# Plan, sampling and MLP regrouped into pairs of tiles shifted by one tile, in an attention-plus-deformable-convolution kernel on one Trainium2 core

## The chip, the cores and the metric

The kernel runs on one core of one Trainium2 chip. The metric is the device time of one execution in microseconds: 3890.51 us is the median of three runs (3889.94 to 3891.61). All arithmetic is in float32.

## The reference

The input is four images of 64 x 64 pixels with 256 channels. Each image goes through two blocks. The first is self-attention over all 4096 pixels of the image, the second a transformer-like block whose spatial step is a deformable convolution with 16 groups of 16 channels and 3 x 3 points.

```python
q, k, v = x @ wq, x @ wk, x @ wv                     # 32, 32 and 256 wide
x = x + gamma * softmax(q @ k.T) @ v                 # 4096 x 4096 in each image
h = ln(x)                                            # layer norm 1
proj = h @ inproj                                    # what is sampled
t = gelu(ln(depthwise3x3(h)))                        # 9 taps, per channel
offset, mask = t @ off_w, softmax(t @ mask_w)        # 16 groups x 9 points
s = sum over points of mask * bilinear(proj, point + offset)
x = x + s @ outproj
x = x + gelu(ln(x) @ fc1) @ fc2                      # 1024 hidden
```

(Biases are left out.) The offsets are small in nearly all places, so the kernel takes the bilinear sample from a window of 5 x 5 pixels around each pixel, with weights (hats) that are zero outside. The few points that fall outside the window are repaired afterwards, in a "far round".

## The kernel before, in words

**Tiles and units.** A tile is 128 pixels, two image rows. A unit is two tiles, 256 pixels. There are 16 units in an image and 64 in all. Everything is done unit by unit, in stages:

- *project* (L407 to L442): q, k and v of one unit of the *next* image: transposes pt_x, the copy xT on ScalarE, the matmuls pkq and pv. Image 0's projection comes ahead of everything.
- *attention* (L502 to L527): scores e in four groups e0 to e3 of 16 matmuls, exponentials ex (steps x0 to x3, four ScalarE instructions each, L515), and the products acc with V (steps w0 to w15 of 8 matmuls each). acc lies in PSUM, two tiles of 257 columns.
- *front* (L543): division by the softmax sum (L550), the residual, layer norm 1 (xn_f, nm_f), transposes pt_f, hT_f, the input projection pp and its store xq to the DRAM tensor xp. Its step scale also stores hT_f to a DRAM image himg (L573).
- *plan* (L607): loads six rows of himg into hs (L613), computes the nine taps into cv (tap 0 on ScalarE, L624, the others on VectorE, L628), transposes to pc, layer norm (xn_p, with rstd_p on GpSimd), gelu, the heads po (L662) and om, the hats, the mask weights, their products pr (L751) and the window weights wn. Its step count puts into cnt how many far points the unit has, with two ScalarE operations named far. It stores am and om to DRAM for the far round.
- *sample* (L830): reads window rows of xp (win) and forms the weighted sum with multiplications (times, L842) and additions (plus, L850, then three across), once per tile and window row. Result sp.
- *back* (L960, which calls finish, L875): transposes pt_s, the output projection pout (L895), the residual x1b, layer norm 2 (xn_b), transposes pt_b, the hidden layer ph (hidden0 to hidden7, L919) with gelu into gT (L927), the second layer pmlp (L936), the store of the output.
- *far round* (L997) once at the end: picks for each of 128 rows a unit with far points, gathers am, om, the table values, four neighbours (nears), sp and x1, and runs them through finish as one tile more. The checks at the end need it.

**Order.** The order is written by hand. `whole` (L1118) gives every step the time slot x 60 + WHEN[stage][step], sorts all steps and emits them in that order, and each of TensorE, VectorE, ScalarE and GpSimd runs its instructions in just that order. SyncE issues the transfers in the same order. Slots are nominal; in the profile a slot takes what its engines need. Attention of unit s has slot s, its front s+1, its plan s+2, its sample and back s+3. So in a steady slot TensorE mixes work of four units and of the next image's projection.

**Buffers.** pt of every kind, ph, pp, pv, pkq, pmlp, pc, po and pout take turns in one PSUM pool of two buffers: each of these tiles can be written only when the one before the last has been read. ScalarE must load another function table when it changes between gelu and exponential; the steps gelu0, gelu1 and exp place a dummy operation (idle, L301) so that the load stands at a chosen place.

The slots of the last stages are set in these lines of `whole`:

```python
put(s + 1, "front", front(att))
put(s + 2, "plan", plan(b, u, wns, general))
put(s + 3, "sample", sample(b, u, wns, sps))
put(s + 3, "back", back(b, u, sps))
```

Of the kernel before, what the change touches and what calls it, by code (L numbers as in the profile page):

```python
# [16 lines left out]
def tile_attention_dcnv3_block(  # L17
# [20 lines left out]

    nc = tc.nc
# [4 lines left out]
    NU = N // 256  # L44
    CQ = wq.shape[1]
# [11 lines left out]
    out_ = out.rearrange("b (t q h2) w c -> b t (h2 w) q c", q=2, h2=2)  # L57
# [110 lines left out]
    himg = []  # L168
    for b in range(B):
        for y in (0, H + 2):  # L170
            nc.gpsimd.dma_start(
                xp[b, y : y + 2].rearrange("y w c -> (y w c)").rearrange("(p f) -> p f", p=P),
                zeros[:, : 2 * WP * C // P],
            )
        for w in (0, W + 2):
            nc.gpsimd.dma_start(
                xp[b, 2 : 2 + H, w : w + 2, :].rearrange("y w c -> y (w c)"), zeros[:H, : 2 * C]
            )
        h = dram.tile([P, C // P, H + 2, W], F32, tag=f"himg{b}", name=f"himg{b}")
        for y in (0, H + 1):  # L180
            nc.gpsimd.dma_start(h[:, :, y, :], zeros[:, : 2 * W].rearrange("p (k w) -> p k w", k=2))
        himg.append(h)

    hs = gp.tile([P, C // P, 6, WP], F32, name="hs")
# [4 lines left out]
    omd = dram.tile([B * NU * P, 2 * NOM], F32, name="omd")  # L189

    amd = dram.tile([B * NU * P, 2 * S], F32, name="amd")
    x1d_ = x1d.rearrange("(u q p) c -> u p q c", q=2, p=P)
    spd_ = spd.rearrange("(u q p) c -> u p q c", q=2, p=P)
    omd_ = omd.rearrange("(u p) m -> u p m", p=P)
    amd_ = amd.rearrange("(u p) m -> u p m", p=P)
# [3 lines left out]

    UN = B * NU  # L200
    tab_s = dram.tile([2 * S, 4], F32, name="tab_s")
    tab_u = dram.tile([UN, 2], F32, name="tab_u")
# [9 lines left out]
    byp = tab[0:1, : 8 * S].rearrange("p (s f) -> p s f", f=4)  # L212
# [3 lines left out]
    numbers(byp[:, :, 3], [[1, 2], [0, S]], 0)  # L216
    nc.vector.scalar_tensor_tensor(byp[:, :, 2], byp[:, :, 3], 2.0, byp[:, :, 2], ALU.mult, ALU.add)
    nc.gpsimd.dma_start(tab_s.rearrange("(o s) f -> o (s f)", o=1), tab[0:1, : 8 * S])
    tab = p1.tile([P, 2 * S], F32, tag="mk", name="tab_b")
    byu = tab[0:1, : 2 * UN].rearrange("p (s f) -> p s f", f=2)  # L220
    numbers(byu[:, :, 0], [[H + 4, B], [0, NU]], 0)
    numbers(byu[:, :, 1], [[0, B], [4, NU]], 0)
    nc.gpsimd.dma_start(tab_u.rearrange("(o s) f -> o (s f)", o=1), tab[0:1, : 2 * UN])
# [9 lines left out]
    rev = gp.tile([P, UN], F32, name="rev")  # L233
    numbers(rev, [[-1, UN]], UN)
# [4 lines left out]
    cnt = gp.tile([P, B * NU], F32, name="cnt")  # L239
# [8 lines left out]
    qd = dram.tile([B * NU, CQ, 256], F32, name="qd")  # L248
# [3 lines left out]
    rall = gp.tile([P, B * NU, 2], F32, name="rall")  # L252
# [53 lines left out]
    def transposed(src, name, n=2, pool=None, tag="m"):  # L306

        pt = (pool or ps).tile([P, C // P, 256], F32, tag=tag, name=f"pt_{name}")
        for k in range(C // P):
# [15 lines left out]
            "load": -8.0, "turn": 14.59, "copy": 19.06, "keys": 20.23, "key_bias": 21.3, "values": 24.48,  # L325
            "value_bias": 27.18,
        },
        "attention": {
            "load": -20.0, "e0": -5.48, "x0": -3.77, "e1": 1.23, "w0": 3.99, "w1": 6.55, "w2": 8.71,
            "w3": 18.86, "x1": 20.1, "e2": 24.15, "x2": 24.96, "w5": 27.12, "e3": 30.32, "w11": 32.05,  # L330
            "w8": 34.09, "w6": 41.58, "w9": 45.95, "w7": 46.83, "w4": 48.34, "x3": 49.31, "w10": 53.77,
            "w12": 54.23, "w14": 54.57, "w13": 56.92, "w15": 60.51,
        },
        "general": {
            "e0": -0.1, "x0": 0.0,
        },
        "tables": {
            "gelu0": -3.72, "gelu1": 34.44, "exp": 43.95,
        },
        "front": {  # L340
            "inverse": 0.67, "residual": 1.94, "stats": 3.81, "shift": 4.26, "norm": 6.3, "turn": 8.65,
            "scale": 10.32, "project_in": 20.46, "store": 24.02, "keep": 37.44,
        },
        "plan": {
            "load": -32.0, "tap0": -4.53, "tap1": -4.08, "tap2": -1.32, "tap3": -0.19, "tap4": 7.76,
            "row": 12.0, "tap5": 16.0, "tap6": 25.94, "tap7": 25.95, "tap8": 25.98, "turn": 28.86,
            "stats": 31.74, "shift": 34.62, "norm": 37.78, "turn2": 39.37, "gelu": 43.09, "heads0": 44.15,
            "bias0": 44.78, "heads1": 44.8, "bias1": 45.25, "mask_exp": 46.47, "hat0": 46.5, "hat2": 48.1,
            "sums": 49.15, "hat1": 49.55, "invert": 50.34, "weigh": 52.55, "nearer": 52.63, "near": 52.66,
            "bounds": 53.75, "mask0": 53.9, "mask1": 54.13, "count": 54.63, "product0": 55.35,  # L350
            "y_copies0": 55.98, "y0": 57.71, "product1": 57.78, "y1": 59.2, "y_copies1": 60.27,
            "x_copies": 60.38, "x": 63.91,
        },
        "sample": {
            "rows01": 4.08, "times01": 4.1, "rows00": 4.39, "times00": 4.41, "rows02": 5.83, "times02": 5.85,
            "plus01": 7.59, "plus02": 10.32, "rows03": 11.62, "times03": 11.64, "rows04": 16.49,
            "times04": 16.51, "plus03": 19.73, "plus04": 24.86, "rows11": 25.7, "times11": 25.72,
            "across00": 25.8, "across01": 28.32, "rows12": 29.39, "times12": 29.41, "across02": 31.4,
            "rows10": 33.28, "times10": 33.3, "plus11": 34.57, "plus12": 37.6, "rows13": 42.08,
            "times13": 42.1, "rows14": 43.6, "times14": 43.62, "plus13": 44.73, "plus14": 46.89,  # L360
            "across10": 49.5, "across11": 50.19, "across12": 51.27,
        },
        "back": {
            "load": 30.0, "turn": 52.73, "copy": 53.52, "project_out": 54.04, "added": 55.57, "stats": 57.22,
            "shift": 57.89, "norm": 59.56, "turn2": 61.2, "scale": 61.21, "raised": 61.31, "hidden0": 62.08,
            "hidden4": 62.46, "gelu0": 63.21, "hidden2": 64.68, "gelu4": 64.68, "gelu2": 64.99,
            "hidden6": 65.94, "hidden1": 67.15, "gelu6": 67.4, "gelu1": 68.64, "hidden5": 69.49,
            "hidden3": 72.49, "gelu5": 72.71, "gelu3": 72.87, "hidden7": 73.81, "gelu7": 77.75,
            "narrowed0": 84.81, "narrowed1": 89.91, "end": 93.7,
        },  # L370
        "far": {
            "unit": -84, "point": -80, "left": -77, "rows": -76, "pixels": -74, "summed": -66, "turn": 34.5,
            "copy": 35.11, "project_out": 35.71, "added": 36.32, "stats": 36.93, "shift": 37.54,
            "norm": 38.14, "turn2": 38.75, "scale": 39.36, "raised": 39.96, "hidden0": 40.57,
            "hidden4": 41.18, "gelu0": 41.79, "hidden2": 42.39, "gelu4": 43.0, "gelu2": 43.61,
            "hidden6": 44.21, "hidden1": 44.82, "gelu6": 45.43, "gelu1": 46.04, "hidden5": 46.64,
            "hidden3": 47.25, "gelu5": 47.86, "gelu3": 48.46, "hidden7": 49.07, "gelu7": 49.68,
            "narrowed0": 50.29, "end": 50.89,
# [164 lines left out]
    def front(att):  # L543
# [26 lines left out]
        def scale():  # L570
            st["hT"] = scaled(st["pt"], g1, b1, f"f{n}")
            for k in range(C // P):
                nc.sync.dma_start(  # L573
                    himg[b][:, k, 1 + 4 * u : 5 + 4 * u, :],
                    st["hT"][:, k, :].rearrange("p (r w) -> p r w", w=W),
                )
# [14 lines left out]
        def store():  # L591
# [11 lines left out]
            "project_in": project_in, "store": store, "keep": keep,  # L603
# [3 lines left out]
    def plan(b, u, wns, general):  # L607
        n = f"{b}_{u}"
        st = {}

        def load(r0, r1):
            for k in range(C // P):
                nc.sync.dma_start(  # L613
                    hs[:, k, r0:r1, 2 : 2 + W], himg[b][:, k, 4 * u + r0 : 4 * u + r1, :]
                )


        def tap(j, k):
            if (j, k) == (0, 0):
                st["cv"] = p1.tile([P, C // P, 256], F32, tag="cv", name=f"cv_{n}")  # L620
            acc = st["cv"][:, k, :].rearrange("p (r w) -> p r w", w=W)
            src = hs[:, k, j // 3 : j // 3 + 4, 1 + j % 3 : 1 + j % 3 + W]
            if j == 0:
                nc.scalar.activation(  # L624
                    acc, src, AF.Identity, bias=dwb[:, k : k + 1], scale=dw[:, k, 0:1]
                )
            else:
                nc.vector.scalar_tensor_tensor(acc, src, dw[:, k, j : j + 1], acc, ALU.mult, ALU.add)  # L628

        def taps(j):  # L630
            tap(j, 0)
            tap(j, 1)

        def turn():
            st["pc"] = ps.tile([P, 2, C], F32, tag="m", name=f"pc_{n}")
            for i in range(2):
# [5 lines left out]
        def stats():  # L642
            statistics(st, [st["pc"][:, i, :] for i in range(2)], f"p{n}")

        def norm():
            normalised(st, [st["pc"][:, i, :] for i in range(2)], f"p{n}")

        def turn2():
            st["pt"] = transposed(st["xn"], f"p_{n}")
# [589 lines left out]
```

## Time and profile before

| quantity | value |
|---|---|
| median of three runs | 3890.51 us |
| the profiled execution | 3889.96 us |
| its span | 3888.1 us |
| a slot of images 0 to 2 in the steady state | 58.2 us |
| a slot of image 3 (no next image to project) | 55.7 us |
| last product with V ends, about | 3691.3 us |

In the profile PE is TensorE and PEld its weight loads, DVE is VectorE, ACT ScalarE, POOL GpSimd, SP SyncE. A row of a timeline gives the start and the length in us, the engine, the line of the kernel, the operation, the tiles written and read (out<-in), the shape, how many instructions were taken together, and in brackets how long the engine had been idle and what ended that. Matmul ends are modelled, so the start of one row to the start of the next is a better measure than a row's length. The busiest groups of the page are these; the last columns are busy us and mean ns of one instruction, then the idle time before them:

```profile
L527 PE MATMUL acc<-V,ex 128*128 128x257 f32 x8192 | 1903.3, 382 | 0.0
...
L842 DVE TENSOR_TENSOR pw<-win,wn 128x1280 f32<-128x1280 f32 x640 | 937.1, 1482 | 7.0 <-ACT gT L927 0.4
L850 DVE TENSOR_TENSOR pw<-pw,pw 128x1280 f32<-128x1280 f32 x512 | 759.2, 1483 | 0.2
L515 ACT ACTIVATE ex<-e 128x512 f32<-128x512 f32 x1024 | 527.4, 600 | 214.3 <-PE e L502 206.7
```

### The profile page before, as it was taken

What the parts mean: (1) busy time and instruction counts of PE and PEld (TensorE: products, weight loads), DVE (VectorE), ACT (ScalarE), POOL (GpSimd) and SP (SyncE); (2) the same over time, 40 slices, a digit from 0 to 9 for tenths busy, and PEclk for the clock granted to TensorE, in tenths of its full rate; (3) what the DMA queues carried; (4) which work ended last, traced back from release to release, by engine and by line L of the source; (5) the groups of instructions that cost most, each with busy time, mean ns of one, the idle gap of its engine ahead of it and who ended that gap; (6) DMA issues with size and microseconds to landing.
All of it is one profiled execution on the core that took longest, in us unless ns stands there. A gap on an engine that the chain in (4) does not pass through costs nothing.

```text
span 3888.1 us, 56223 instructions
## 1 busy us (share of the span) xinstructions
PE 3783.9 (97%) x20284; PEld 3120.9 (80%) x20284; DVE 3413.4 (88%) x6157; ACT 1996.0 (51%) x3986; POOL 320.0 (8%) x445
## 2 busy tenths in 40 slices
PE   8999999999999999999999999999999999999946
PEld 7878888888888888888888888888888888888834
DVE  2399989989989989989989989999999999999995
ACT  4555555555555555555555555555555555555522
POOL 2000000000000000000000000000000000000020
PEclk9999999999999999999999999999999999999977
DMA  5343343335343334334444334334435333433331
GB/s 148 91 117 100 107 111 103 104 111 149 102 131 106 102 110 107 100 111 120 132 130 110 99 109 111 99 108 113 135 99 129 97 101 99 107 97 103 93 89 32
DMA packets 352352, 419.95 MB, mean 108 GB/s; under 512 B 137312, under 2 KB 302368, under 8 KB 352064
## 3 DMA queue, kind: packets, MB, share of 16 engines
q1 hardware_dynamic: 341904, 409.42, 39.0%
q10 hardware_dynamic: 8512, 3.43, 0.4%
q8 instruction: 162, 2.65, 0.3%
q0 software_dynamic: 1648, 3.40, 0.3%
q14 instruction: 126, 1.03, 0.1%
HBM read 276.86 MB, written 139.27 MB: 107 GB/s over the span
## 4 chain that ended last, share of the span: by engine, by line
PE 95%; DVE 4%; DMA 1%; issue 0%; ACT 0%; POOL 0%; SPq 0%; POOLq 0%; ACTq 0%; DVEq 0%
PE acc L527 46%; PE ph L919 11%; PE pmlp L936 11%; PE e L502 7%; PE po L662 5%; PE pv L434 3%; PE pout L895 3%; PE pp L586 3%; PE pkq L413 1%; DVE pw L842 1%; PE pc L638 1%; PE pt_s L311 1%; PE pt_p L311 1%; PE pt_f L311 1%; PE pt_b L311 1%; PE pt_x L311 1%
## 5 line engine op out<-in xcount | busy, mean ns | idle before, releaser
L527 PE MATMUL acc<-V,ex 128*128 128x257 f32 x8192 | 1903.3, 382 | 0.0
L527 PEld LDWEIGHTS acc<-V,ex 128*128 128x128 f32 x8192 | 1528.5, 190 | 261.0 <-issue 64.8
L842 DVE TENSOR_TENSOR pw<-win,wn 128x1280 f32<-128x1280 f32 x640 | 937.1, 1482 | 7.0 <-ACT gT L927 0.4
L850 DVE TENSOR_TENSOR pw<-pw,pw 128x1280 f32<-128x1280 f32 x512 | 759.2, 1483 | 0.2
L515 ACT ACTIVATE ex<-e 128x512 f32<-128x512 f32 x1024 | 527.4, 600 | 214.3 <-PE e L502 206.7
L919 PE MATMUL ph<-hT_b,f1w 128*128 128x256 f32 x2048 | 496.5, 386 | 3.2 <-ACT hT_b L291 2.7
L927 ACT ACTIVATE gT<-ph,f1b 128x256 f32<-128x256 f32 x512 | 241.2, 471 | 478.2 <-PE ph L919 478.2
L936 PE MATMUL pmlp<-f2w,gT 128*128 128x256 f32 x2048 | 466.6, 381 | 0.0
L919 PEld LDWEIGHTS ph<-hT_b,f1w 128*128 128x128 f32 x2048 | 384.8, 192 | 80.9 <-issue 20.1
L628 DVE SCALAR_TENSOR_TENSOR cv<-hs,dw,cv 128x256 f32<-128x256 f32 x1024 | 436.7, 478 | 6.3 <-ACT cv L624 6.3
L936 PEld LDWEIGHTS pmlp<-f2w,gT 128*128 128x128 f32 x2048 | 384.6, 191 | 54.9 <-issue 5.3
L283 ACT ACTIVATE xn_p<-pc,nm_p,rstd_p 128x256 f32<-128x256 f32 x128 | 65.2, 560 | 615.6 <-DVE nm_p L275 615.6
L502 PE MATMUL e<-qs,kT 32*128 32x256 f32 x4096 | 305.5, 402 | 0.7 <-ACT ex L515 0.7
L502 PEld LDWEIGHTS e<-qs,kT 32*128 32x128 f32 x4096 | 191.9, 184 | 86.2 <-issue 53.1
L301 ACT ACT_TABLE_LOAD x192 | 246.3, 1283 | 2.6
L269 POOL TENSOR_SCALAR rstd_p<-mv_p 128x2 f32<-128x2 f32 x64 | 81.5, 1274 | 1562.3 <-DVE mv_p L267 1562.3
L662 PE MATMUL po<-om_w,ge 128*128 128x432 f32 x512 | 199.4, 533 | 1.3 <-ACT ge L655 1.3
L751 DVE TENSOR_TENSOR pr<-hat 128x1296 f32<-128x1296 f32 x128 | 192.5, 1504 | 6.7
L593 DVE TENSOR_TENSOR xq<-pp,inb 128x512 f32<-128x512 f32 x64 | 44.2, 691 | 138.8 <-PE pp L586 138.8
L662 PEld LDWEIGHTS po<-om_w,ge 128*128 128x128 f32 x512 | 98.5, 193 | 73.0 <-issue 57.2
L434 PE MATMUL pv<-wv_s,xT 128*128 128x256 f32 x512 | 127.7, 393 | 4.0 <-DVE V L442 4.0
L269 POOL TENSOR_SCALAR rstd_b<-mv_b 128x2 f32<-128x2 f32 x64 | 20.8, 325 | 1311.7 <-DVE mv_b L267 1290.7
(211 smaller groups left out, 3683.4 us busy)
## 6 DMA issues: line engine op xcount, KB each, us to landing
win<-xp SPq DMA_DIRECT2D x536, 320.0 KB, 4.5
omd<-om SPq DMA_DIRECT2D x64, 432.0 KB, 2.8
hs<-himg SPq DMA_DIRECT2D x128, 160.0 KB, 3.1
xs<-in_x_dram SPq DMA_DIRECT2D x64, 256.0 KB, 2.9
x<-in_x_dram SPq DMA_DIRECT2D x64, 256.0 KB, 2.9
himg<-hT_f SPq DMA_DIRECT2D x128, 128.0 KB, 2.9
xp<-xq SPq DMA_DIRECT2D x128, 128.0 KB, 2.4
x1d<-x SPq DMA_DIRECT2D x64, 256.0 KB, 3.2
```

The source lines that it names most:

```text
L301: nc.scalar.activation(idle, minus_half[:, 0:1], func)
L434: nc.tensor.matmul(pv[:, i, :], lhsT=st["xT"][:, k, i * P : (i + 1) * P], rhs=wv_s[:, k, :], start=(k == 0), stop=(k == 1),)
L502: nc.tensor.matmul(es[r][:, jj, :], lhsT=self.kT[2 * g + jj][rows4(r), :], rhs=self.qs[rows4(r), :], start=True, stop=not self.general,)
L515: nc.scalar.activation(ex, self.es[r], AF.Exp)
L527: nc.tensor.matmul(self.acc[i], lhsT=ex[:, jj, i * P : (i + 1) * P], rhs=V[t // 2][:, t % 2, :], start=(g == 0 and r == 0 and jj == 0), st ...
L628: nc.vector.scalar_tensor_tensor(acc, src, dw[:, k, j : j + 1], acc, ALU.mult, ALU.add)
L662: nc.tensor.matmul(st["po", i], lhsT=st["ge"][:, k, i * P : (i + 1) * P], rhs=om_w[:, k, :], start=(k == 0), stop=(k == 1),)
L842: nc.vector.tensor_mul(st[r].rearrange("p d (g c) -> p (d g) c", c=GC), src.rearrange("p d (g c) -> p (d g) c", c=GC), wns[b, u][:, i, r] ...
L850: nc.vector.tensor_add(st[0], st[0], st[r])
L919: nc.tensor.matmul(ph[:, :m], lhsT=f1w[:, k, c * P : (c + 1) * P], rhs=st["hT"][:, k, :m], start=(k == 0), stop=(k == 1),)
L927: nc.scalar.activation(st["gT"][:, c, :m], st["ph", c][:, :m], AF.Gelu, bias=f1b[:, c : c + 1])
L936: nc.tensor.matmul(po, lhsT=st["gT"][:, c, i * P : (i + 1) * P], rhs=f2w[:, c, :], start=(c == 0), stop=(c == NH - 1),)
```

## The change

Attention and front still go by units. Plan, sample and back go by pairs v = 0 to 64: pair v holds the tiles 2v-1 and 2v, so pairs 0 and 64 hold one tile each, and a pair at a border of images (v = 16, 32, 48) holds the last tile of one image and the first of the next. Pair v needs pixel rows only up to the first half of unit v and one row more, which front of unit v yields. Plan of pair v has slot v+1, the slot of that front, and sample and back have slot v+2.

The DRAM image himg goes, with its stores, loads and zero fills. hs has seven rows and stays in SBUF: the new step image copies hT_f into rows 3 to 6 on ScalarE, and the new step carry moves the rows 4 to 6 down to 0 to 2 after the taps. The centre tap comes first and is the one on ScalarE. A tap that would read over the border of two images is cut in two. am, om and the window weights are stored by pairs, with four zero fills for the missing tiles of pairs 0 and 64; the far round picks pairs, and reads the image and row of a tile from a table by tiles, with one more small gather moved from its step pair to point.

All times in WHEN are new, for project and attention too. Among them: pt_x stands between hidden2 and hidden4, and pv ahead of pkq; hidden3 comes late, after most of the products with V; count comes in the next slot, among the gelus. With the new places of gelu and exponential there are six table loads in a steady slot instead of four.

```diff
+    def tiles_of(v):
+        return max(2 * v - 1, 0), 1 if v in (0, UN) else 2
...
-    hs = gp.tile([P, C // P, 6, WP], F32, name="hs")
+    hs = gp.tile([P, C // P, 7, WP], F32, name="hs")
...
         "project": {
-            "load": -8.0, "turn": 14.59, "copy": 19.06, "keys": 20.23, "key_bias": 21.3, "values": 24.48,
-            "value_bias": 27.18,
+            "load": -14.4, "turn": 19.72, "copy": 23.24, "values": 37.05, "value_bias": 42.74, "keys": 48.45,
+            "key_bias": 50.49,
...
         "tables": {
-            "gelu0": -3.72, "gelu1": 34.44, "exp": 43.95,
+            "gelu0": -12.71, "gelu1": 13.84, "exp": 41.13,
...
-            "shift": 57.89, "norm": 59.56, "turn2": 61.2, "scale": 61.21, "raised": 61.31, "hidden0": 62.08,
-            "hidden4": 62.46, "gelu0": 63.21, "hidden2": 64.68, "gelu4": 64.68, "gelu2": 64.99,
-            "hidden6": 65.94, "hidden1": 67.15, "gelu6": 67.4, "gelu1": 68.64, "hidden5": 69.49,
-            "hidden3": 72.49, "gelu5": 72.71, "gelu3": 72.87, "hidden7": 73.81, "gelu7": 77.75,
-            "narrowed0": 84.81, "narrowed1": 89.91, "end": 93.7,
+            "shift": 59.05, "norm": 59.26, "raised": 59.37, "turn2": 59.4, "scale": 59.75, "hidden0": 59.78,
+            "hidden5": 61.44, "gelu0": 65.24, "gelu5": 67.65, "hidden1": 68.95, "gelu1": 70.18,
+            "hidden2": 73.18, "gelu2": 77.76, "hidden4": 81.06, "gelu4": 84.59, "hidden6": 84.61,
+            "hidden7": 87.12, "gelu6": 87.36, "gelu7": 93.93, "hidden3": 99.62, "gelu3": 101.35,
+            "narrowed0": 102.2, "narrowed1": 106.29, "end": 106.65,
...
         def scale():
             st["hT"] = scaled(st["pt"], g1, b1, f"f{n}")
-            for k in range(C // P):
-                nc.sync.dma_start(
-                    himg[b][:, k, 1 + 4 * u : 5 + 4 * u, :],
-                    st["hT"][:, k, :].rearrange("p (r w) -> p r w", w=W),
-                )
+
+        def image():
+            nc.scalar.copy(hs[:, :, 3:, 2 : 2 + W], st["hT"].rearrange("p k (r w) -> p k r w", w=W))
...
+            dy = j // 3 - 1
+            parts = [(0, 4)]
+            if v % NU == 0 and dy:
+                parts = [(0, 2), (3, 4)] if dy < 0 else [(0, 1), (2, 4)]
+            r0 = 2 if v == 0 else 0
+            for a, b in parts:
+                a, b = max(a, r0), min(b, r0 + 2 * nt)
+                if a >= b:
+                    continue
+                src = hs[:, k, a + 1 + dy : b + 1 + dy, 1 + j % 3 : 1 + j % 3 + W]
+                dst = acc[:, a - r0 : b - r0, :]
...
+        def carry():
+            nc.scalar.copy(hs[:, :, :3, 2 : 2 + W], hs[:, :, 4:, 2 : 2 + W])
...
-                put(s + 2, "plan", plan(b, u, wns, general))
-                put(s + 3, "sample", sample(b, u, wns, sps))
-                put(s + 3, "back", back(b, u, sps))
+        for v in range(PN):
+            put(v + 1, "plan", plan(v, wns, general))
+            put(v + 2, "sample", sample(v, wns, sps))
+            put(v + 2, "back", back(v, sps))
...
-            put(B * NU + 2, "far", far_round(B * NU - 3))
-            put(B * NU + 2, "checks", checks)
+            put(UN + 2, "far", far_round(UN - 3))
+            put(UN + 2, "checks", checks)
```

## The prediction

> **What bounds the kernel now.** I read the page's totals, slices and chain first, then a table of two typical stretches, then single rows where two numbers did not fit, then the tail.
>
> ```profile
> span 3888.1 us, 56223 instructions
> ...
> PE 3783.9 (97%) x20284; PEld 3120.9 (80%) x20284; DVE 3413.4 (88%) x6157; ACT 1996.0 (51%) x3986; POOL 320.0 (8%) x445
> ...
> PEclk9999999999999999999999999999999999999977
> ...
> PE 95%; DVE 4%; DMA 1%; issue 0%; ACT 0%; POOL 0%; SPq 0%; POOLq 0%; ACTq 0%; DVEq 0%
> ```
>
> TensorE holds 95% of the chain, and no queue or transfer holds more than 1%: only what shortens PE's own sequence, or PE's waits at the two ends, can move the time. The profiled run took 3889.96 us, 1.9 over its span and 0.55 under the median; the sum below is made on 3889.96.
>
> The next view is busy time by stage: one attention slot of image 1 and one of image 3.
>
> ```profile
> 1520.49:1578.71 58.22, 58.22 (x318) 48.27 (x317) 52.90 (x94) 30.86 (x63) 4.40 (x6) 1.00 0.38 106
> ...
> 3302.59:3358.30 55.71, 55.71 (x301) 45.91 (x300) 52.31 (x93) 29.30 (x59) 4.40 (x6) 1.00 0.38 101
> ```
>
> The columns are length, busy PE, PE's weight loads, DVE, ACT and POOL, granted clock, DMA share and GB/s. PE fills both slots, and DVE has 5.3 and 3.4 us left. An image-3 slot lacks the next image's projection: pt_x 0.44, pkq 0.86 and pv 1.73 us from start to start, 3.03 in all. It is only 2.51 shorter, so 0.52 us hide in it. The timeline of PE (start, us) shows where; one row from either slot, and the one after:
>
> ```profile
> 1539.60 1.15 PE L502 MATMUL e<-qs,kT 32*128 32x256 f32 x16
> ...
> 3320.40 1.67 PE L502 MATMUL e<-qs,kT 32*128 32x256 f32 x16
> 3322.00 3.72 PE L936 MATMUL pmlp<-f2w,gT 128*128 128x256 f32 x16
> ```
>
> Start to start the same 16 matmuls take 1.08 us in image 1 and 1.60 in image 3. ScalarE's timeline gives the reason:
>
> ```profile
> 3317.05 0.47 ACT L927 ACTIVATE gT<-ph,f1b 128x256 f32<-128x256 f32 x1 [0.39 <-PE ph L919]
> 3317.53 1.28 ACT L515 ACT_TABLE_LOAD   x1
> 3318.82 2.06 ACT L515 ACTIVATE ex<-e 128x512 f32<-128x512 f32 x4
> ```
>
> The four exponentials of e1 end at 3320.88, and e2 needs the PSUM they free. Without the projection PE is there too early, and waits inside a row that counts as busy.
>
> The tail, from the last acc (3691.3) to the end at 3888.1, is 196.8 us. Its windows and waits of PE:
>
> ```profile
> 3700.00:3750.00 50.00, 19.81 (x69) 13.62 (x68) 43.45 (x112) 6.57 (x13) 18.37 (x14) 0.74 0.37 91
> 3750.00:3800.00 50.00, 28.91 (x93) 20.32 (x93) 47.33 (x80) 16.11 (x33) 4.36 (x5) 0.78 0.30 83
> ...
> 3850.00:3889.00 39.00, 22.77 (x91) 17.83 (x89) 3.95 (x10) 6.48 (x13) 2.04 (x3) 0.82 0.06 20
> ```
> ```profile
> PE pt_s L311 <- DVE sp L859: 15.4, 3, 9.9
> PE pt_b L311 <- ACT xn_b L283: 15.0, 4, 6.0
> PE pc L638 <- DVE cv L628: 14.8, 2, 7.7
> PE pt_s L311 <- DVE om L671: 9.2, 1, 9.2
> ```
>
> Here DVE leads, PE waits for it, and PE's granted clock falls to 0.74 to 0.82.
>
> **The change part by part.** All sums follow the changed order of each engine, with the durations of the rows of before.
>
> *A steady slot: PE.* Plan, sample and back keep their matmuls; only their grouping into units moves by a tile. The floor stays 58.2 us with the projection and 55.2 without, and PE's order has no operation more. Cost 0 as long as each producer ends before PE asks.
>
> *A steady slot: DVE.* 64 taps of 256 elements and all else stay; a tap is cut in two only at the four image borders. 53 us against 58.2 is cover enough. In image 3 it is 52.5 against 55.2; without that cover each us of DVE over 55.2 would cost 16.
>
> *A steady slot: ACT.* Added: the copy of hT into the row buffer (128x512; the like copy xT takes 0.58) and the carry of three rows (384 elements, between us 0.31 and xT 0.58, so 0.45), and table loads go from 4 to 6 a slot (the order alternates more between gelu and exp), 2.57. ACT rises from 31 to 35 us of 58, with most of it beside PE.
> Here a rule speaks against the change. The Trainium skill ("ScalarE: Activation LUTs", section "What ACT_TABLE_LOAD costs") charges a switch with the 1283 ns load and a further 1380 ns of drain, 2.66 in all. The rows above show the load starting 0.01 us after gT ends, and the first exponential 1.29 after the load starts: no drain is seen. By the row the first gelu of a slot is ready 0.7 us before ph1 asks for its buffer (ledger: 4.45 against 5.17 us after pt_b). By the rule it would be 1.4 later, 0.7 too late in 64 slots: +45 us. I take the row.
>
> *A steady slot: PSUM.* ph, pt, pc, po, pp, pv, pout, pkq and pmlp share two buffers in turn, so each waits until the one before the last was read. In the new order pt_x stands amid the hidden layers, and ph6 must wait for the copy xT, which queues on ACT behind gT1, two far counts (0.54 and 0.44), a table switch's idle (0.20), gT2 and two xn_f (0.52 each at pitch). The ledger ends xT at 9.65 to 9.9 us after pt_b, and PE wants ph6 at 9.94. Behind ph6 all of PE's slot queues. Bounds: the 0.52 us of the one ACT wait of this kind in the trace, and −0.24, because PE's pitches add up to 57.97 of the 58.22 and the new order might save the difference. As the estimated slack is 0 to 0.3, I take +0.05 a slot, in the 48 slots with a projection: +2.4. The other slacks in the ledger are 0.2 to 0.5 us (heads after gelu, pt_s after sp, pout after sT): 0.
>
> *Image 3.* The exponentials of e1 now end 3 to 5 us before e2 asks, since e2 stands later in the order. The 0.52 goes in 16 slots: −8.3. Next late is po after ge, 0.3 us of slack.
>
> *Transfers.* The DRAM image goes: 128 stores (128 KB, 2.9 us to land) and 128 loads with their row loads (160 KB, 3.1). They lay beside PE with queues at 39%: gain 0. Plan, sample and back take their transfers with them (am, om, the window rows, sp, x1, out); in SP's order none of these stands in front of a load that is due earlier: 0, and if one did, times, with 5 us of DVE's room in a slot, would hide it. Eight zero fills by GpSimd become four, before the first slot: 0.
>
> *The head.* DVE-bound slots fill the pipeline. The slot at 186.5 to 239.8 took 53.3 us, and its PE records add up to 43.7 at pitch: 9.6 lost. With plan one slot earlier, taps delay pc by about 5.6 in slot 2, and slot 3 (PE 50.9, DVE 53.5) loses 2.6: 8.2. Gain 1.4, with 0.5 of waits for xn_p that no longer occur: −1.9, bounds −5 to +3.
>
> *The tail and what leaves it.* When the last acc ends there remain 3.5 backs, 2.5 samples and 1.5 plans instead of 4, 3 and 2. Half a pair's PE work therefore moves ahead of it: 32 matmuls of the MLP at 0.217 (6.9), half of pout 0.87, one po 1.45 and transposes 0.9 to 1.0: +10.2 in a stretch that PE fills. The tail of before by its DVE rows: to the add of f2b at 3762.06 70.3 us; to the next at 3812.82 50.8; to the end of the last sum 40.2; the last back 26.6; its end 8.5 and 0.4 between.
> After: the first stretch keeps two tiles everywhere (70.1), but the plan's rstd queues on POOL behind four gathers of the far round: POOL is busy 18.4 us in that window, and my queue count makes nm_p about 3.3 late, so 73.4. The second has half a plan: 42.2 of DVE records, and 5.1 of waits (pout at the low clock 3.1, twice 0.5, and 1.1): 47.3. Then the MLP of pair 63 is the path and no longer DVE, 19.2; the far round's one-tile back 16.3 (18.0 in before, 1.7 of it a wait for DVE); the last back has one tile and is like the far one, 17.0 instead of 26.6; end 8.5. Sum 181.7 against 196.8: −15.1, bounds −18 to −10.
>
> Sum: 3889.96 + 2.4 − 8.3 − 1.9 + 10.2 − 15.1 = 3877.3, and 0.55 to the median: **3878 us**, 0.3% faster.
>
> **The rivals.**
> *The stall moves instead of going.* In image 3 DVE has 2.7 us left and po 0.3. If a new wait of 0.52 takes the place of the old, −8.3 is lost; with xT at 0.1 a slot (+2.4 more) it ends at 3889. For it: every link in the order is tight. Against it: the largest known wait has 3 us of slack.
> *The xT copy decides; slower.* If ph6 waits 0.52 a slot, the size that image 3 shows for an ACT wait, 48 × 0.52 = 25 instead of 2.4: 3901. It turns the gain into a loss from 0.31 us a slot (15/48). For it: no slack in the ledger and three ACT operations of another stage ahead. Against it: the sum uses whole durations, and gT rows follow each other at 0.44 or less.
> *The tail does better.* No wait on POOL (−3.3), no wait for xT (−2.4), the second stretch without its pout wait (−3.1), the head at −5: 3866; two us more if part of the 0.24 falls away.
>
> **How the numbers follow.** A change of 0.2%, 7.8 us, is about what a measurement of this kernel can tell from none: 3882.7 and 3898.3 are the borders. The likeliest case has 0.58 (3870 to 3886 with the tail's, head's and xT's bounds), the better tail 0.14, the moved stall 0.18, the slow case 0.10. Faster: most of the first, 0.54, and the second, with 0.06 of the third: 0.74. Slower: most of the fourth, 0.08. The rest, 0.18, is within. The range from 3864 to 3889 leaves the slow case and half of the moved stall out.
>
> **What would show it.** Slots of 58.2 in images 0 to 2 (58.7 would be the slow case, and ph6 rows long by 0.5) and 55.2 in image 3, with e2 at 1.15 us; 6 table loads a slot with ex 1.29 after the load's start; no himg transfers; the last acc near 3694 (3691.3 + 10.2 + 2.4 − 8.3 − 1.9); then about 182 us of tail, with the far chain behind the MLP of pair 63. The prediction fails if a slot is not PE's, or if the new tail is led by something that I took for covered, POOL above all.

## The result, and the profile after

The changed kernel takes 3876.2 us (median of six runs, 3874.87 to 3878.25) against 3890.41 us (six runs, 3888.19 to 3891.61): a ratio of 0.9964, 95% interval 0.9951 to 0.9977. The forecast was 3878. The profiled execution has a span of 3874.4 us and took 3876.21.

The page of the changed kernel, the lines that answer to those of before:

```profile
span 3874.4 us, 55924 instructions
...
PE 3777.5 (97%) x20316; PEld 3125.1 (81%) x20316; DVE 3424.4 (88%) x6224; ACT 2204.0 (57%) x4262; POOL 317.5 (8%) x444
...
PEclk9999999999999999999999999999999999999977
...
PE 94%; DVE 4%; DMA 1%; issue 0%; ACT 0%; POOL 0%; ACTq 0%; POOLq 0%; DVEq 0%
```

ScalarE is 208 us busier and the chain has not noticed: it is still 94% PE. Busy time by stage, one slot of image 1 and one of image 3 (length, busy PE, PEld, DVE, ACT, POOL, clock, DMA share, GB/s):

```profile
1531.50:1589.71 58.21, 58.21 (x317) 48.38 (x316) 53.07 (x94) 34.13 (x66) 4.40 (x6) 1.00 0.34 95
3364.03:3419.22 55.19, 55.19 (x302) 45.72 (x301) 52.20 (x93) 32.60 (x62) 4.41 (x6) 1.00 0.32 90
```

The first slot is as long as before, to 0.01 us, with 3.3 us more on ScalarE. The second is 0.52 shorter. Its row of e2 on TensorE, and on ScalarE the exponentials of e1 that it needs:

```profile
3383.57 1.15 PE L506 MATMUL e<-qs,kT 32*128 32x256 f32 x16
3384.65 2.00 PE L531 MATMUL acc<-V,ex 128*128 128x257 f32 x8
```
```profile
3376.80 0.47 ACT L936 ACTIVATE gT<-ph,f1b 128x256 f32<-128x256 f32 x1
3377.28 1.28 ACT L519 ACT_TABLE_LOAD   x1
3378.57 2.06 ACT L519 ACTIVATE ex<-e 128x512 f32<-128x512 f32 x4
```

The exponentials end at 3380.6, and TensorE comes 2.9 us later: e2 takes 1.08 us from start to start, no longer 1.60. The table load again starts 0.01 us after the gelu ends, and the exponential 1.29 after that.

The tail, from the end of the last acc (3694.8) to 3874.4, is 179.6 us, 17.2 shorter. Its windows and TensorE's waits in it:

```profile
3700.00:3750.00 50.00, 24.44 (x81) 16.94 (x80) 44.99 (x112) 10.28 (x21) 19.06 (x14) 0.69 0.34 86
3750.00:3800.00 50.00, 28.66 (x91) 19.59 (x89) 48.48 (x87) 16.29 (x36) 4.19 (x5) 0.76 0.24 67
3800.00:3850.00 50.00, 35.75 (x145) 27.82 (x145) 28.22 (x58) 14.81 (x35) 3.05 (x5) 0.76 0.06 19
```
```profile
PE pc L648 <- DVE cv L635: 19.3, 2, 13.9
PE pt_b L316 <- ACT xn_b L288: 13.9, 3, 5.4
PE pt_p L316 <- ACT xn_p L288: 12.1, 2, 8.9
PE pt_s L316 <- DVE sp L868: 7.1, 2, 4.5
```

VectorE leads until 3800, and is only 28 us busy in the third window: there the chain of MLPs leads. Over the whole tail VectorE's busy time fell from 148.5 to 128.3 us, as half a pair less to do would have it.

### The profile page after: what moved, and what is told of

It reads as the page before. It is cut to its first block, busy times and chain, and to the rows that moved or that the text cites. A ratio compares the mean times of both kernels' runs of the same rounds, so it can differ in the third digit from the quotient of the medians.

```text
span 3874.4 us, 55924 instructions
## 1 busy us (share of the span) xinstructions
PE 3777.5 (97%) x20316; PEld 3125.1 (81%) x20316; DVE 3424.4 (88%) x6224; ACT 2204.0 (57%) x4262; POOL 317.5 (8%) x444
## 4 chain that ended last, share of the span: by engine, by line
PE 94%; DVE 4%; DMA 1%; issue 0%; ACT 0%; POOL 0%; ACTq 0%; POOLq 0%; DVEq 0%
PE acc L531 46%; PE ph L928 11%; PE pmlp L945 11%; PE e L506 7%; PE po L672 5%; PE pout L904 3%; PE pv L438 3%; PE pp L588 3%; PE pkq L417 1%; DVE pw L851 1%; PE pt_s L316 1%; DVE pw L859 1%; PE pt_p L316 1%; PE pt_b L316 1%; PE pc L648 1%; PE pt_f L316 1%
## 5 line engine op out<-in xcount | busy, mean ns | idle before, releaser
L928 PE MATMUL ph<-hT_b,f1w 128*128 128x256 f32 (+1 forms) x2080 | 497.8, 383 | 4.2 <-ACT hT_b L296 2.5
L635 DVE SCALAR_TENSOR_TENSOR cv<-hs,dw,cv 128x256 f32<-128x256 f32 (+1 forms) x1076 | 427.6, 462 | 7.5 <-ACT cv L631 1.5
L288 ACT ACTIVATE xn_p<-pc,nm_p,rstd_p 128x256 f32<-128x256 f32 x128 | 65.4, 560 | 608.2 <-DVE nm_p L280 608.2
L936 ACT ACTIVATE gT<-ph,f1b 128x256 f32<-128x256 f32 (+1 forms) x520 | 236.2, 467 | 241.2 <-PE ph L928 240.0
L506 PE MATMUL e<-qs,kT 32*128 32x256 f32 x4096 | 295.7, 401 | 0.7 <-ACT ex L519 0.7
L274 POOL TENSOR_SCALAR rstd_p<-mv_p 128x2 f32<-128x2 f32 (+1 forms) x65 | 80.4, 1237 | 1680.3 <-DVE mv_p L272 1680.2
L665 ACT ACTIVATE ge<-pt_p,bd,gd 128x256 f32<-128x256 f32 (+1 forms) x130 | 65.9, 558 | 161.3 <-PE pt_p L316 161.3
L672 PEld LDWEIGHTS po<-om_w,ge 128*128 128x128 f32 x512 | 98.5, 193 | 72.8 <-issue 64.4
L681 DVE TENSOR_TENSOR om<-po,om_b 128x432 f32<-128x432 f32 x128 | 77.4, 604 | 88.2 <-PE po L672 88.2
```

Of the source, the lines that this page charges most:

```text
L506: nc.tensor.matmul(es[r][:, jj, :], lhsT=self.kT[2 * g + jj][rows4(r), :], rhs=self.qs[rows4(r), :], start=True, stop=not self.general,)
L635: nc.vector.scalar_tensor_tensor(dst, src, dw[:, k, j : j + 1], dst, ALU.mult, ALU.add)
L672: nc.tensor.matmul(st["po", i], lhsT=st["ge"][:, k, i * P : (i + 1) * P], rhs=om_w[:, k, :], start=(k == 0), stop=(k == 1),)
L928: nc.tensor.matmul(ph[:, :m], lhsT=f1w[:, k, c * P : (c + 1) * P], rhs=st["hT"][:, k, :m], start=(k == 0), stop=(k == 1),)
L936: nc.scalar.activation(st["gT"][:, c, :m], st["ph", c][:, :m], AF.Gelu, bias=f1b[:, c : c + 1])
```

## The experiments

Theory: the time is 16 image-3 waits that are gone, and a tail with half a pair less to do, minus the half pair of TensorE work that moved ahead of it; the other slots, the transfers and ScalarE's extra work are neutral. Rivals: the lighter queues bring part of it; the image-3 gain comes from the grouping and not from a wait; the PSUM turn at ph6 is not the edge it was taken for.

**e2 later, in the kernel before.**

```diff
-"e2": 24.15, "x2": 24.96
+"e2": 24.9, "x2": 24.96
```

> The kernel before with one number changed: e2 moves behind the first half of the second layer (and behind pv), so that TensorE reaches it 3.5 us later and the exponentials of e1 have ended. Theory (a wait for x1 hides in each image-3 slot): image-3 slots go from 55.70 to 55.18, slots of images 0 to 2 stay at 58.21, time 3890.4 - 15 or 16 x 0.52 = 3882.4. Rival (the shorter image-3 slot of the changed kernel comes from the regrouping into pairs, or from the transfers that are gone): slots stay at 55.70 and the time at 3890.

Measured: 3937.9 us, 47 slower. The image-3 slots did fall, to 55.40. But images 0 to 2 rose to between 59.3 and 59.4, which I had not expected. There pv moved ahead of e2 too, and now met the PSUM turn: it waits for qT, the reader of pkq, which stands behind the exponentials. The same row in the timeline of TensorE:

```profile
1569.48 1.99 PE L434 MATMUL pv<-wv_s,xT 128*128 128x256 f32 x8 [0.79 <-ACT qT L427]
```

A swap of two steps that are both "not waiting" costs 1.1 us a slot. So the edit was repeated for image 3 alone:

```diff
+                if b == B - 1:
+                    steps.append((s * T + 24.9, len(steps), some.pop("e2")))
                 put(s, "attention", some)
```

> The kernel before with e2 moved behind the first half of the second layer in image 3 alone, so that the projection's use of the PSUM buffers in images 0 to 2 is not touched. In the run that moved it everywhere the image-3 slots came to 55.40. Theory (a wait for the exponentials of e1 hides there; 0.22 of its 0.52 us turn up again at pc, which then waits for VectorE's last taps): slots of 58.21 and 55.40, 3890.5 - 16 x 0.31 = 3885.6. Rival (nothing hides there): 3890.5.

Measured: 3886.3 us (3882.8 to 3888.6), ratio to before 0.9990 (0.9982 to 0.9998); slots are 58.21 and 55.40, as expected. The wait is real and has nothing to do with pairs. TensorE's rows there show where the rest stays:

```profile
3375.34 1.15 PE L502 MATMUL e<-qs,kT 32*128 32x256 f32 x16
3376.41 2.00 PE L527 MATMUL acc<-V,ex 128*128 128x257 f32 x8
3378.25 0.81 PE L638 MATMUL pc<-ident,cv 128*128 128x128 f32 x4
3378.90 3.40 PE L936 MATMUL pmlp<-f2w,gT 128*128 128x256 f32 x15
```

e2 now takes 1.07, but pc 0.65 from start to start and not 0.44: it waits for the last taps on VectorE, whose row ends at 3378.46. In the old order 0.31 of the 0.52 was to be had; the changed kernel, whose taps come early, has all of it.

**The copy xT, later in the changed kernel**, by one operation or by waiting for ph4.

```diff
-"carry": 60.61
+"carry": 82.0
```

> The changed kernel with the step carry (0.51 us on ScalarE, 0.42 at pitch) moved from before the slot's gelus to just ahead of the copy xT. The trace of the changed kernel has xT end 9.6 us after pt_b and ph6 start at 9.94, a slack of 0.33. Theory (the second user of a PSUM buffer is the sharp edge of the new order, as the slow rival of the prediction had it): 0.42 less 0.33 is 0.1 us of wait or, with the latency of the semaphore, up to 0.2, in 48 slots: 3876.2 + 5 to 10 = 3881 to 3886, slots of images 0 to 2 at 58.3 to 58.4, image 3 unchanged at 55.18. Rival (the wait is taken up by TensorE's queue or the slack is larger than it looks): 3876.

Measured: 3887.1 us (3885.4 to 3891.5), 10.9 more, which gives back three quarters of the gain; the ratio to the kernel before is 0.9993 (0.9985 to 1.0001). Slots of images 0 to 2 are 58.46, 0.25 longer, and 48 x 0.25 = 12. On ScalarE (in this kernel's slot pt_b began at 2706.87) and on TensorE:

```profile
2715.91 0.51 ACT L642 COPY hs<-hs 128x384 f32<-128x384 f32 x1
2716.32 0.58 ACT L411 COPY xT<-pt_x 128x512 f32<-128x512 f32 x1
```
```profile
2714.20 1.90 PE L531 MATMUL acc<-V,ex 128*128 128x257 f32 x8
2715.94 3.01 PE L928 MATMUL ph<-hT_b,f1w 128*128 128x256 f32 x12
2718.78 0.60 PE L316 MATMUL pt_f<-ident,xn_f 128*128 128x128 f32 x4
```

No idle time is printed; the wait sits inside ph's row, 2.84 us from start to start and not 2.59. As 0.42 of delay cost 0.25, the changed kernel had 0.17 us in hand. The slow rival's mechanism is real; it does not bind by 0.17 us.

```diff
-"copy": 23.24
+"copy": 24.6
```

> The changed kernel with the copy xT moved behind gelu4 on ScalarE. gelu4 must wait for ph4, which ends 9.94 us after pt_b, so xT ends near 11.2 and ph6, which TensorE reaches at 9.94, can start near 11.4. Theory (that buffer is the edge): 1.4 us in each of 48 slots, 3876.2 + 67 = 3943, slots of images 0 to 2 at 59.6. Rival (another operation of TensorE's order fills in, or later waits shrink by as much): well under 30 us more.

Measured: 3911.9 us, 35.7 more, half of the 67 expected. Slots are 59.05, 0.83 longer. The rows of ph4 and ph6 on TensorE, and of gelu4 and xT on ScalarE, tell why:

```profile
2736.65 1.03 PE L928 MATMUL ph<-hT_b,f1w 128*128 128x256 f32 x4
2738.24 1.99 PE L928 MATMUL ph<-hT_b,f1w 128*128 128x256 f32 x8 [0.56 <-ACT gT L936]
```
```profile
2737.72 0.47 ACT L936 ACTIVATE gT<-ph,f1b 128x256 f32<-128x256 f32 x1 [0.99 <-PE ph L928]
2738.09 0.58 ACT L411 COPY xT<-pt_x 128x512 f32<-128x512 f32 x1
```

ph6 starts at 2738.24, when gelu4 has just ended (2738.19) and xT has not (2738.67). So it waits for gelu4, not for xT. The reading that fits is that in this order it took the buffer of ph4 and left pt_x's to ph7; the rows do not name the buffers. The two buffers, then, do not always go strictly in turn, and "the one before the last", as the buffers were described, is the usual case only.

**The removed transfers put back** (stores and loads of the old sizes, the loads into DRAM).

```diff
...
+            for k in range(C // P):
+                nc.sync.dma_start(
+                    himg[b][:, k, 1 + 4 * u : 5 + 4 * u, :],
+                    st["hT"][:, k, :].rearrange("p (r w) -> p r w", w=W),
+                )
...
+                    nc.sync.dma_start(himc[:, k, 0:4, :], himg[v // NU][:, k, 4 * (v % NU) + 1 : 4 * (v % NU) + 5, :])
+                    nc.sync.dma_start(himc[:, k, 4:6, :], himg[v // NU][:, k, 4 * (v % NU) + 3 : 4 * (v % NU) + 5, :])
```

> The changed kernel with the removed transfers put back as dead work: two stores of hT per unit to a DRAM image as before, and four loads of six rows from it in the step carry, into a second DRAM buffer and not into SBUF. Nothing reads them. Theory (the transfers lay beside TensorE): 3876, slots 58.21 and 55.18. Rival (a part of the gain comes from lighter queues): several us more, up to the 14 that were gained.

Measured: 3877.0 us (3876.6 to 3878.9), slots 58.21 and 55.18. Its main queue moves 409.4 MB, as in the kernel before (367.5 in the changed one), and the DMA share of a slot is back at 0.38. The bytes were worth nothing. The packets are not all back, 276,704 against 341,904, for the old loads ended in the padded rows of hs. What those packets cost was not tested.

**The far round's place in the tail.** First GpSimd's queue: pixels moved behind nm_p.

```diff
-"pixels": -74
+"pixels": -72.7
```

> The changed kernel with the far round's step pixels moved behind nm_p of the plan in the last slots, so that rstd_p no longer queues on GpSimd behind the four gathers. Theory (the gathers delay rstd_p, VectorE then idles 1.95 us ahead of nm_p, and the tail is VectorE's): about 2 us less, 3874. Rival (pixels itself, 5 us on VectorE, only changes place, and the gathers now land too late for summed): 3876 to 3879.

Measured: 3873.7 us (3873.1 to 3874.1). The first stretch of the tail, from pt_b to pt_b, went from 69.26 to 67.06 us as expected, but the next grew by 0.7 and the rest by 1.1. The tail is 179.1 instead of 179.6; the last acc ends 2.0 us earlier, which is within what the start of the program varies by (below). The growth need not come from the edit: the runs with the carry later and with the transfers put back, whose far round stands where it was, show it too, with 49.4 and 49.5 us in the second stretch instead of 48.4, and 63.0 in the rest instead of 61.9. In these three runs the granted clock in the rest is 0.77, in the changed kernel 0.80. The 2.2 us are a gain in the first stretch; what the whole program keeps of them is not shown. That rstd_p queues behind the gathers is shown by VectorE's row of the changed kernel:

```profile
3742.19 0.16 DVE L280 SCALAR_TENSOR_TENSOR nm_p<-mv_p,rstd_p 128x2 f32<-128x2 f32 x1 [1.95 <-POOL rstd_p L275]
```

Then the far round left out of the main pass, in both kernels (one line of `whole` deleted).

> The kernel before with the far round left out of the main pass (its far points are then left to the general repair at the end, which runs only where some are left). Theory: 18.0 us of the far round's own chain on TensorE and some 16 to 18 of VectorE's work in the first stretch of the tail go: 3890.4 - 34 = 3856 if the repair loop does not run; a loop run would add tens of us. Rival (the far round is hidden): 3885 or more.

> The changed kernel with the far round left out of the main pass. Theory (the far round costs both kernels the same, and the shorter tail comes from half a plan, half a sample and half a back fewer behind the last product with V): 3876.2 - 33 = 3843, so 13 less than the kernel before without its far round. Rival (part of the gain in the tail is the far round's new order, picks by pairs and one gather moved): the two kernels without far rounds differ by less than 9.

Measured: 3924.9 and 3900.4 us. The repair did run: from the end of the last regular pmlp to the end it is 59.5 and 63.3 us, where the full kernels need 9.2 and 10.4. So it adds some 50 us to both, and the times themselves say little. From the traces, last acc to end of the last regular pmlp: 170.9 us before and 142.5 after. With the far round the same stretch is 187.6 and 169.2. So the far round costs the old kernel 17 us and the changed one 27: my theory of an equal cost is wrong. In the first stretch it costs both about the same, 15.1 and 14.0 us; from the third pt_b of the tail to the last one it costs 4.0 and 13.2. VectorE's last sum sp in the kernel before and in the changed one shows the reason:

```profile
3852.24 0.42 DVE L942 TENSOR_TENSOR f_x_f<-f_x_f,pmlp_f 128x256 f32<-128x256 f32 x1 [3.30 <-PE pmlp_f L936]
3852.58 0.42 DVE L859 TENSOR_TENSOR sp<-pw 128x256 f32<-128x256 f32 x1
```
```profile
3832.99 0.43 DVE L868 TENSOR_TENSOR sp<-pw 128x256 f32<-128x256 f32 x1
...
3847.89 0.42 DVE L951 TENSOR_TENSOR f_x_f<-f_x_f,pmlp_f 128x256 f32<-128x256 f32 x1 [10.54 <-PE pmlp_f L945]
```

Before, the far tile's MLP lay beside the last sampling, and both ended together. In the changed kernel the last pair has one tile, its sum is ready 15 us before the far tile is through, and the far tile stands alone on the path. A gain of 28 us in the tail's regular work came out as 18.

**The far tile earlier.** The experiment that this points to takes that tile through projection and MLP in the waits of the stretch before.

```diff
-"turn": 46.75, "copy": 47.03, "project_out": 47.31, ... "narrowed0": 54.05, "end": 54.33
+"turn": -13.3, "copy": -13.25, "project_out": -11.2, ... "narrowed0": -1.7, "end": 2.0
```

> The changed kernel with the far round's tile taken through projection and MLP about 50 us earlier: in the gaps that TensorE has in the last but one stretch of the tail (its waits for pc, xn_p, sp and xn_b there are 5.4, 3.1, 4.5 and 5.4 us). Theory (that tile costs 16 us only because it stands alone on the path, one chain behind another): 11.6 us of its TensorE work go into gaps, 3 to 5 come back as delays of pt_s and pt_b: 3876.2 - 12 = 3864. Rival (VectorE, 97% busy in that stretch, or the table loads on ScalarE delay the plan of the last pair by as much): 3872 to 3880.

Measured: 3865.0 us (3861.2 to 3866.3), 0.9936 of the kernel before (0.9922 to 0.9950): 11 below the changed kernel. The tail is 171.3, so 8.3 us of this are the far tile's, and not the 12 of the theory; the rest of the difference between the two profiles, 3.3 us, lies ahead of the end of the last acc, where nothing was changed. That the median met the theory is in part luck. pt_b of pair 63 comes 6.9 us later after the last acc than without, more than the 3 to 5 that I had set.

**Two attempts at more**, which also defer om_w and om_b past the start.

> The changed kernel with the early far tile of a_far_early, and with the loads and reorderings of the head weights and biases (om_w, om_b) taken out of the start: their transfers queue ahead of the first image tiles on SyncE, and the copies of the biases stand ahead of V on VectorE (TensorE waits 7.7 us for the first tile and 5.0 for V). Theory: the 4 to 5 us of the second wait and about 1 of the first go, 3865.0 - 5 = 3860, e0 starts near 60 instead of 64 to 67 us. Rival (other loads take their place): 3863 to 3866.

> As a_best, with the far tile another 4 to 10 us earlier: its projection before pc of the last pair, its hidden layers between the second layer of pair 62 and pt_s of pair 63, where a_far_early still delayed pt_b of pair 63 by 7 us. Theory (there is room in the waits for pc, xn_p and sp): another 3 to 5 us less, 3856. Rival (the far tile then delays the heads of the last pair and with them VectorE, which is full there): 3860 to 3866.

Measured: 3867.4 (3863.3 to 3870.7) and 3866.7 (3863.4 to 3867.3): no gain over 3865.0. The theories fail; both medians lie about 1 us above the rivals' ranges. The first tile comes earlier (TensorE begins at 4.7 and 5.5 us and not at 7.7) and V no longer waits for the copies, but pv waits 1.6 us for wv and pkq up to 4.0 for xT; and the tail of the second is 171.4, since pt_b_f now waits 6.6 us for its layer norm and pt_b of pair 63 comes 0.9 us earlier only.

## Why the prediction was right, step by step

- *Steady slots, +2.4 for ph6 behind xT.* Measured 0: slots of 58.21 in both. The ledger's time for xT was right (9.65 to 9.9 us after pt_b; the trace has 9.61), and ph6 starts at 9.94. The 0.17 us that the experiment found in hand lies in the foretold 0 to 0.3. My 0.05 a slot was a hedge, and nothing of it appeared. VectorE has 16 taps of 256 elements in a slot of either kernel, not the 64 that the prediction names; as their number does not change, the sum is untouched.
- *ScalarE's two more table loads.* There are 386 loads instead of 262, six and four a slot. No drain shows in the rows above, and ph1 has no wait: the row of 8 matmuls that it begins takes 1.72 us from start to start, as without a wait. The figure of 2.66 us per switch that the Trainium skill states ("ScalarE: Activation LUTs", "What ACT_TABLE_LOAD costs") would have cost some 45 us by the prediction's estimate; the measured slot shows nothing of it, so the row was the right one to take.
- *Image 3, −8.3.* Fifteen slots of 55.18 instead of 55.70 give −7.8. The last slot has no next attention and came 0.4 us longer than its counterpart: −7.4. No wait is left there, for 55.18 is 58.21 less the 3.03 of the projection.
- *The head, −1.9.* Up to the first steady slot (pt_b at 239.74 and 250.81 us) the profile shows +11.1 instead of 10.2 − 1.9 = 8.3; of these two terms only the sum can be read. But e0 begins at 67.08 us in the profile after and at 64.41 in that of before. This need not be part of the change: with the same code for the start, the runs made from the changed kernel begin e0 between 64.2 and 67.5, and five of these seven at 64.2 to 65.4, like all four profiles made from the old kernel (64.4 to 65.2). Take these 2.7 off, and 8.4 is left.
- *Transfers, 0.* Measured 0.
- *The tail, −15.1.* Measured −17.2. The first stretch ends with f2b 69.85 us after pt_b and not 73.4. This is the term that was mis-sized. rstd_p does wait some 4 us on GpSimd, but VectorE has other work ready and idles 1.95, and without that wait the stretch is only 2.2 us shorter, not 3.3. The other 2.4 us are in the 70.1 that was carried over from before, VectorE's other waits included. Most of that is one wait, for the far round's first gather, which is 2.1 us shorter in the changed kernel. In the kernel before and in the changed one:

```profile
3729.16 0.46 DVE L1031 SCALAR_TENSOR_TENSOR f_am_f<-f_am_f,f_sid_f 128x288 f32<-128x288 f32 x1 [3.40 <-DMA f_am_f<-amd,ints]
```
```profile
3717.19 0.46 DVE L1041 SCALAR_TENSOR_TENSOR f_am_f<-f_am_f,f_sid_f 128x288 f32<-128x288 f32 x1 [1.34 <-DMA f_am_f<-amd,ints]
```

  The second stretch, from f2b to f2b, took 48.3 (47.3 foretold), the rest 61.5 (61.0).

The sum by the profiles: 2.7 + 8.4 − 7.4 − 17.2 = −13.5, with 0 for the slots, and the spans differ by 13.7. The mechanism was right, part by part. That the forecast came within 2 us is also luck, for its errors cancel: the slots (−2.4) and the tail (−2.1) came out shorter than foretold, the start (+2.7) and image 3 (+0.9) longer. No run separates the grouping into pairs from the new order and times of the steps: that the shorter tail comes from half a pair less work rests on the sum and on VectorE's busy time.

The rivals: the moved stall did not come, for the changed kernel has no wait left in image 3, though the old order, patched, kept 0.21 of 0.52 at pc. Of the better tail, the whole 2.4 for xT and 1.1 of the 3.3 for GpSimd came true. The xT rival missed by 0.17 us a slot; at +0.25 it cancelled three quarters of the gain. That the far tile's cover is lost was not among my rivals. Its cost was in the sum, as a piece of 16.3 on the path, but that this piece could be moved only became plain with the far round left out.

## What to carry to other kernels

When an engine is full, look for waits inside its busy rows: compare the same row from start to start in two stages, and ask what the longer one is waiting for. In an order that is written by hand, a step that shares a scarce PSUM buffer can decide: a quarter of a microsecond in each of 48 slots cost here three quarters of what the redesign had brought, and a swap of two steps that both seem free can cost more than it brings. In a tail, a shorter main chain uncovers what lay beside it; measure each side chain by leaving it out, then move it into the waits.

## What was not expected

The same start takes between 64.2 and 67.5 us until e0 from one profiled run to the next, with TensorE waiting for the first tile and for V or wv. The tail varies too: in the changed kernel and the three variants that leave the far round alone (carry later, xT behind gelu4, transfers back) it takes 179.6, 181.4, 179.9 and 181.9 us. Each is as large as several of the terms argued about here. Which of the two makes the spread of 3 us between the runs of one kernel is not shown, as only one run of each has a trace. Times that differ by less than 3 us are better compared from a mark inside the trace.

A wait of a matmul was printed as idle time in some places ([0.56 <-ACT gT]) and hidden in the row's length in others (ph 0.25 longer, e2 0.52, pc 0.21). Idle time alone would have shown none of the three waits on which this case turned.
